# Four tiles' left-over rows of the experts' way down, taken together in 32-row products

## The chip, the cores and the metric

The kernel runs on one core of a Trainium2 chip. A core has a matrix engine (TensorE, PE in the profile; its weight loads are PEld), a vector engine (DVE), a scalar engine (ACT), a general engine (GpSimd, POOL) and a queue engine that issues DMAs (SyncE, SP). The engines run side by side, each in the order of its own instructions, and wait for one another with semaphores. Data lies in SBUF (128 partitions), and products go to PSUM, eight banks of 512 float32 values a partition. The metric is the device time of one execution, in microseconds (us).

## The reference

One decoder layer in float32 on 32 sequences of 128 tokens of width 512: self-attention with two softmaxes a head, cross-attention with rotary embeddings, and a mixture of experts with a shared expert. The change touches the experts alone:

```python
B, S, H = hidden_states.shape                     # 32, 128, 512
E, K = (NUM_EXPERTS, TOP_K)                       # 32 experts, 6 of them for each token
x = hidden_states.reshape(-1, H)                  # 4096 tokens
scores = jax.nn.sigmoid(x @ gate_w)
...                                               # the best 2 of 4 groups, then the best 6 experts
xs = x_exp[sort_idx]                              # 24576 rows, sorted by expert
g = jax.lax.ragged_dot(xs, w_gate, group_sizes)   # w_gate: 32 x 512 x 352
u = jax.lax.ragged_dot(xs, w_up, group_sizes)
d = jax.lax.ragged_dot(jax.nn.silu(g) * u, w_down, group_sizes)   # w_down: 32 x 352 x 512
expert_out = jnp.sum(out * weights[..., None], axis=1)
```

The inner width M is 352, which is two times 128 and 96.

## The kernel before

The stages follow one another: self-attention, cross-attention, routing, and then the experts, between groups of the shared expert. The routing sorts the rows into 192 tiles of 128 rows of one expert each (`usual`), and 8 shared tiles whose two halves of 64 rows belong to two experts (`mixed`). One shared tile stands after every 24 tiles, ahead of a tile whose number is a multiple of four.

An expert's weights lie in one of four sets of buffers (`SETS = 4`): tile i uses set i mod 4, and a load is skipped where the set holds the expert already (`cond=new`). `wg` and `wu` hold gate and up, `wd` holds the way down as three chunks of rows: 128, 128 and 96.

`Experts.run` writes the order of work out by hand, for PE, DVE, ACT and POOL, step by step. In step k of the loop:

- `gate_up(k)` (L1598): PE multiplies the tile's turned inputs `e_xT` by gate and up, four products of 128x352 each, into two PSUM banks; ACT takes silu of the first (L1602), DVE multiplies by the second into the one buffer `e_gu` (L1603).
- `turn_in_place(k)` (L1620): DVE turns two of the four 96-column parts of `e_gu` in 32x32 blocks, all 128 lanes at once, into `e_turned`.
- `turn_in(k + 2)` (L1584): DVE turns the fetched token rows `e_xr` of the tile two ahead into `e_xT`, four turns of 64x256. There are two buffers of `e_xT`.
- `turn_out(k)` (L1609): DVE turns the other two parts straight into their partitions of `e_guT`, eight turns of 32x96.
- `weights_in(k + 4)` (L1543): SP issues the loads of gate and up.
- `down(k - 2)` (L1637): PE multiplies `e_guT` by `wd`, three products of 512 columns, into one bank; ACT scales the result into `e_out` (L1641), and POOL issues the scatter that adds its rows to `sum_d` in HBM (L1644).
- `weights_out(k + 2)` (L1555, L1558): SP issues the two loads of `wd`.
- `move_out(k)` (L1627): ACT copies `e_turned` to its partitions of `e_guT`, eight copies.
- `tokens(k + 5)` (L1569): POOL issues two indirect fetches of token rows.

Every float32 product shows in the profile as two passes of PE, each with its own weight load. PSUM is handed out in pairs of banks, four pairs in turn (`Common.banks`). The shared tile's products use 64 columns of the array for each half. After the loop the engines pass a branch (L1831, further tiles if there are more than 192, which are none here), and the last groups of the shared expert follow (`Shared.group`, L1265 to L1304). These have 64 rows left over of 704 and take them for two blocks side by side (L1304). Cross attention has products of 32 rows and 512 columns, a head each, in different 32-row groups of the array (L690, L713).

Of the kernel before, what the change touches and what calls it, by code (L numbers as in the profile page):

```python
# [10 lines left out]
F32 = mybir.dt.float32  # L11
# [1303 lines left out]
class Experts:  # L1315
# [13 lines left out]
    RUN = 96  # L1329

    def __init__(
# [19 lines left out]
        self.wd = [cp.tile([P, len(M_CHUNKS), E], F32, name=f"wd{s}") for s in range(SETS)]  # L1351
# [92 lines left out]
    def fetch_halves(self):  # L1444
# [3 lines left out]
            self.p2.tile([P, len(M_CHUNKS), P], F32, name="e_guT", bufs=3)[0:32]  # L1448
# [98 lines left out]
    def weights_out(self, i):  # L1547

        if i not in self.expert:
            return  # L1550
        e, new = self.expert.pop(i)
        wd, src = self.wd[i % SETS], self.w_out[ds(e, 1)]
        top = (self.Q - 1) * 32
        m = (self.Q - 1) * self.RUN
        self.cm.nc.sync.dma_start(  # L1555
            out=wd[0:top], in_=src[:, 0:m, :].rearrange("o (p c) m -> p (o c) m", p=top), cond=new
        )
        self.last = self.cm.nc.sync.dma_start(  # L1558
            out=wd[top:P, 0:2, :], in_=src[:, m:M, :].rearrange("o (p c) m -> p (o c) m", c=2),
            cond=new,  # L1560
        )
# [43 lines left out]
    def turn_out(self, i):  # L1605
        t, half = self.guT[i], self.Q // 2
        for q in range(half):
            for s in range(self.Q):
                self.cm.nc.vector.transpose(t[ts(q, 32), :, ts(s, 32)], self.part(q, 3)[ts(s, 32)])  # L1609

    def part(self, q, n):
        return self.gu_s[:, ds(q * self.RUN, 32 * n)].rearrange("p (j c) -> p c j", c=n)

    def turn_in_place(self, i):
        half = self.Q // 2
        self.guT[i] = self.p2.tile([P, len(M_CHUNKS), P], F32, name="e_guT", bufs=3)
        z = self.turned[i] = self.p2.tile([P, half, len(M_CHUNKS), 32], F32, name="e_turned")
        for q in range(half, self.Q):
            n = min(self.RUN, M - q * self.RUN) // 32
            self.cm.nc.vector.transpose(z[:, q - half, 0:n], self.part(q, n))  # L1620

    def move_out(self, i):
        half, z, t = self.Q // 2, self.turned.pop(i), self.guT[i]
        for q in range(half, self.Q):
            n = min(self.RUN, M - q * self.RUN) // 32
            for s in range(self.Q):
                self.cm.nc.scalar.copy(t[ts(q, 32), 0:n, ts(s, 32)], z[ts(s, 32), q - half, 0:n])  # L1627

    def down(self, i):
        nc = self.cm.nc  # L1630
        py = self.cm.banks()[:, 0, :]
        t, last = self.guT.pop(i), len(M_CHUNKS) - 1
        both = [slice(0, P)] if i < self.n_tiles else [ts(h, P // 2) for h in range(2)]
        w = [self.wd[i % SETS]] if i < self.n_tiles else self.xd
        for c, (_, n) in enumerate(M_CHUNKS):
            for lanes, wd in zip(both, w):
                nc.tensor.matmul(  # L1637
                    py[lanes], t[:n, c, lanes], wd[:n, c, :], start=c == 0, stop=c == last
                )
        y = self.p3.tile([P, E], F32, name="e_out", bufs=4)  # L1640
        nc.scalar.mul(y, py, self.weight[:, i : i + 1])  # L1641
        m = i - self.n_tiles
        for into in [self.into[:, i : i + 1]] if m < 0 else [self.into_half[:, h, m : m + 1] for h in range(2)]:
            nc.gpsimd.indirect_dma_start(  # L1644
# [24 lines left out]
    def run(self):  # L1669
# [8 lines left out]
        with self.cm.tc.manual_schedule(engines={en.PE, en.DVE, en.Activation, en.Pool}):  # L1678
# [5 lines left out]
            for k in range(len(seq) + 2):  # L1684
# [5 lines left out]
                each(self.down, k - 2)  # L1690
                each(lambda i: self.weights_out(i + SETS), k - 2)
                each(self.move_out, k)
                if k < gap // 2 or k % 2:
                    next(loads, None)
                each(self.tokens, k + 5)
                m = seq[k - 2] - self.n_tiles + 1 if 2 <= k < len(seq) + 2 else 0
                if 0 < m < self.mixed:
                    loads = self.mixed_loads(m)
# [200 lines left out]
```

## Time and profile before

| | us |
|---|---|
| median of 3 runs | 3797.29 |
| lowest, highest | 3795.77, 3797.58 |
| the profiled execution, whole | 3800.08 |
| the profiled execution, span of instructions | 3798.3 |

The granted clock of PE was 0.992 of full speed over the span. The totals of the engines, and where the experts' tiles lie:

| stretch (us from the span's start) | PE busy | DVE busy | ACT busy | POOL busy |
|---|---|---|---|---|
| 2000 to 2100, the experts begin | 95.17 | 65.97 | 29.47 | 40.75 |
| 2100 to 2300 | 200.00 | 157.51 | 87.78 | 102.76 |
| 2900 to 3100 | 200.00 | 157.63 | 87.80 | 102.51 |
| 3300 to 3500, they end | 199.19 | 150.59 | 87.08 | 91.41 |
| 3500 to 3700, shared expert | 197.32 | 22.01 | 13.31 | 3.08 |

Busy time is the time in which an engine had at least one instruction in work. A row of the profile names the source line, the engine, the operation, the tiles (written <- read), the shape and the count; then come busy time and the mean length of one in ns, and the idle time before it with the engine that ended it. Matmuls overlap with their followers in the pipeline, so the step from one start to the next tells what a pass costs, and not its length. `32*128` ahead of a product's shape says how many rows and columns of the array it takes.

### The profile page before, as it was taken

The page shows a single profiled execution, that of the slowest core. Times are in us where ns is not written, and L with a number is a line of the kernel's source. Part 1 is how long each engine was busy: PE and PEld are TensorE (multiplying, and loading weights), DVE is VectorE, ACT ScalarE, POOL GpSimd, SP SyncE. Part 2 cuts the span into 40 slices and gives each one's busy share as a digit, 9 for nine tenths or more (in the row PEclk, how much of TensorE's full clock was granted, in tenths as well). Part 3 has the DMA queues.
Part 4 walks back from the last instruction along what each step waited for, and adds up shares of the span by engine and source line. Part 5 has one row for each costly group of instructions (what it writes and reads, how often), then busy time and mean ns, then how long its engine had stood idle before and what let it go on. Part 6 is the DMA issues. An engine that isn't in the chain of part 4 may idle for free. (4 is left out here: it accounts for less than half of the span.)

```text
span 3798.3 us, 59896 instructions
## 1 busy us (share of the span) xinstructions
PE 3717.0 (98%) x19060; PEld 1967.8 (52%) x19060; DVE 2677.8 (70%) x5402; ACT 2076.4 (55%) x5616; POOL 1917.2 (50%) x2154
## 2 busy tenths in 40 slices
PE   8999999899999999999999999999999999999999
PEld 5666666534444444444445555555555555555444
DVE  4888888877777778787326777777777777776111
ACT  6989998847677676776402444444444444443000
POOL 3555455545777777777424554555555555553000
PEclk9999999999999999999999999999999999999999
DMA  3111110121221111111135565656566665564210
GB/s 113 34 35 35 35 37 30 39 83 49 62 60 42 51 51 51 48 49 40 56 110 169 128 164 134 166 121 164 122 156 142 150 150 141 135 172 81 89 56 33
DMA packets 146548, 340.25 MB, mean 90 GB/s; under 512 B 28976, under 2 KB 33776, under 8 KB 146160
## 3 DMA queue, kind: packets, MB, share of 16 engines
q1 hardware_dynamic: 89408, 227.75, 18.8%
q0 software_dynamic: 55616, 107.79, 15.4%
q8 instruction: 154, 2.52, 0.3%
q14 instruction: 170, 1.39, 0.1%
q10 hardware_dynamic: 1200, 0.79, 0.1%
HBM read 574.59 MB, written 102.17 MB: 178 GB/s over the span
## 5 line engine op out<-in xcount | busy, mean ns | idle before, releaser
L694 DVE TENSOR_REDUCE nm<-ps 128x2 f32<-128x1024 f32 x512 | 610.6, 1214 | 113.2 <-PE ps L690 106.8
L717 ACT ACTIVATE xp<-ps 128x1024 f32<-128x1024 f32 x512 | 505.8, 1021 | 264.5 <-PE ps L690 202.7
L1644 POOL DMA_INDIRECT sum_d<-e_out,e_into x192 | 309.9, 1614 | 562.6 <-ACT e_out L1641 438.4
L713 PE MATMUL ps<-xqn,xk 32*128 32x512 f32 x2048 | 528.9, 621 | 20.7 <-ACT xp L717 19.1
L1637 PE MATMUL ps<-wd,e_guT 128*128 128x512 f32 (+1 forms) x1152 | 526.9, 593 | 0.3 <-ACT e_guT L1627 0.3
L690 PE MATMUL ps<-xk,xq 32*128 32x512 f32 x2048 | 526.9, 631 | 0.1
L1584 DVE STREAM_TRANSPOSE e_xT<-e_xr 64x256 f32<-64x256 f32 x800 | 499.5, 624 | 18.9 <-DMA e_xr<-h_d,e_run_of 10.7
L1609 DVE STREAM_TRANSPOSE e_guT<-e_gu 32x96 f32<-32x96 f32 x1600 | 477.7, 299 | 25.2
L1569 POOL DMA_INDIRECT e_xr<-h_d,e_run_of x400 | 413.8, 1035 | 159.7 <-issue 150.0
L1598 PE MATMUL ps<-wg,e_xT 128*128 128x352 f32 x1536 | 486.7, 459 | 0.0
L1598 PE MATMUL ps<-wu,e_xT 128*128 128x352 f32 x1536 | 485.7, 459 | 0.0
L1627 ACT COPY e_guT<-e_turned 32x96 f32<-32x96 f32 (+1 forms) x1600 | 407.1, 254 | 25.1 <-DVE e_turned L1620 3.9
L1598 PEld LDWEIGHTS ps<-wg,e_xT 128*128 128x128 f32 x1536 | 289.7, 189 | 217.8 <-issue 94.5
L278 ACT ACTIVATE s<-s,a_nm 128x128 f32<-128x128 f32 x1024 | 395.7, 396 | 5.2 <-DVE a_nm L264 5.2
L1598 PEld LDWEIGHTS ps<-wu,e_xT 128*128 128x128 f32 x1536 | 291.8, 190 | 162.6
L1641 ACT ACTIVATE e_out<-ps,e_weight 128x512 f32<-128x512 f32 x200 | 137.4, 687 | 411.8 <-PE ps L1637 409.5
L1637 PEld LDWEIGHTS ps<-wd,e_guT 128*128 128x128 f32 (+1 forms) x1152 | 218.5, 190 | 228.2 <-issue 188.5
L1602 ACT ACTIVATE e_act<-ps 128x352 f32<-128x352 f32 x200 | 92.6, 463 | 412.7 <-PE ps L1598 412.7
L713 PEld LDWEIGHTS ps<-xqn,xk 32*128 32x128 f32 x2048 | 169.0, 184 | 285.5 <-ACT xp L717 124.5
L1603 DVE TENSOR_TENSOR e_gu<-e_act,ps 128x352 f32<-128x352 f32 x200 | 104.1, 521 | 274.6 <-ACT e_act L1602 274.1
L728 PE MATMUL ps<-xp,v 128*32 128x512 f32 x2048 | 233.0, 595 | 7.9 <-ACT xp L717 7.9
L1031 POOL DMA_INDIRECT table_d<-entry,at x192 | 202.4, 1054 | 64.0 <-issue 52.9
(310 smaller groups left out, 5575.4 us busy)
## 6 DMA issues: line engine op xcount, KB each, us to landing
wg<-in_L_ffn_w_gate_dram SPq DMA_DIRECT2D x192, 704.0 KB
wu<-in_L_ffn_w_up_dram SPq DMA_DIRECT2D x192, 704.0 KB
wd<-in_L_ffn_w_down_dram SPq DMA_DIRECT2D x192, 576.0 KB
wd<-in_L_ffn_w_down_dram SPq DMA_DIRECT2D x192, 128.0 KB
xg<-in_L_ffn_w_gate_dram SPq DMA_DIRECT2D x16, 704.0 KB
xu<-in_L_ffn_w_up_dram SPq DMA_DIRECT2D x16, 704.0 KB
xd<-in_L_ffn_w_down_dram SPq DMA_DIRECT2D x16, 576.0 KB
xres<-in_x_dram SPq DMA_DIRECT2D x32, 256.0 KB
```

What stands on the lines that cost most here:

```text
L278: nc.scalar.activation(s[:, j, c, side, :], s[:, j, c, side, :], AF.Exp, bias=nm[n][:, side, at : at + 1], accum_out=sm[n][:, to : to + 1],)
L690: self.nc.tensor.matmul(sc[:, i, :], q[rows, ts(c, P)], k[rows, :], start=True, stop=True)
L694: self.nc.vector.tensor_reduce(at[:, self.ROW[side], 2 * pair : 2 * pair + 2], sc, AX.X, ALU.max, negate=True)
L713: self.nc.tensor.matmul(sc[:, i, :], k[rows, ts(c, P)], q[rows, :], start=True, stop=True)
L717: self.nc.scalar.activation(e, sc, AF.Exp)
L1569: self.cm.nc.gpsimd.indirect_dma_start(out=xr[:, t, :], out_offset=None, in_=self.h3_d.rearrange("t (h f) -> (t h) f", h=self.R), in_offse ...
L1584: self.cm.nc.vector.transpose(to[ts(w, half), :, v], xr[ts(v, half), w])
L1598: nc.tensor.matmul(pgu[lanes, half, 0:M], t[:, c, lanes], w[:, c, :], start=c == 0, stop=c == EC - 1,)
L1609: self.cm.nc.vector.transpose(t[ts(q, 32), :, ts(s, 32)], self.part(q, 3)[ts(s, 32)])
L1627: self.cm.nc.scalar.copy(t[ts(q, 32), 0:n, ts(s, 32)], z[ts(s, 32), q - half, 0:n])
L1637: nc.tensor.matmul(py[lanes], t[:n, c, lanes], wd[:n, c, :], start=c == 0, stop=c == last)
L1644: nc.gpsimd.indirect_dma_start(out=self.sum_d[:, :], out_offset=bass.IndirectOffsetOnAxis(ap=into, axis=0), in_=y[:, :], in_offset=None, b ...
```

## The change

The way down of a tile is split. Its first 256 rows are two full products, as before. Its last 96 rows are laid out over 32 partitions, three deep, in the 32-row group of the tile's set (its lane): partitions 32s to 32s + 31 for set s. The weights of these rows go to one buffer `wd_ends` for the four sets, and the turned activations of four tiles to one buffer `e_endT`. The way down is then done once for a group of four tiles: eight full products, and three rounds of four 32-row products, each in its own row group and into its tile's own PSUM bank, added to what the full products left there. It stands after the gate and up of the tile two behind the group's last one.

With it go these moves. The tile's columns are cut in four parts of 64 and one of 96. DVE turns parts 0 and 1 outward as 32x64 (eight turns), and three parts in place (two of 64 columns and the 96). ACT makes twelve copies for a tile instead of eight, the last four into the tile's lane of `e_endT`. `move_out` stands ahead of the way down in the step. The four results of a group leave together (`leave`), and the scatters are issued two a step from a list (`ready`). The loads of `wd` and `wd_ends` for the next four tiles are issued together after the group. The shared tiles keep their three products (`down_shared`).

```diff
@@ -1327,6 +1327,7 @@
     Q = 4
     R = 2
     RUN = 96
+    FULL, LEFT = 2, 3
 
     def __init__(
         self, cm, ctx, table_ds, h3_d, sum_d, w_gate, w_up, w_down, eid, fresh, rows, n_tiles,
@@ -1348,7 +1349,9 @@
         self.NT = rows.shape[1]
         self.wg = [cp.tile([P, EC, M], F32, name=f"wg{s}") for s in range(SETS)]
         self.wu = [cp.tile([P, EC, M], F32, name=f"wu{s}") for s in range(SETS)]
-        self.wd = [cp.tile([P, len(M_CHUNKS), E], F32, name=f"wd{s}") for s in range(SETS)]
+        self.wd = [cp.tile([P, self.FULL, E], F32, name=f"wd{s}") for s in range(SETS)]
+        self.ends = cp.tile([P, self.LEFT, E], F32, name="wd_ends")
+        self.py, self.endT = {}, {}
 
         self.gu_s = cp.tile([P, M], F32, name="e_gu")
 
...
@@ -1549,15 +1552,14 @@
         if i not in self.expert:
             return
         e, new = self.expert.pop(i)
-        wd, src = self.wd[i % SETS], self.w_out[ds(e, 1)]
-        top = (self.Q - 1) * 32
-        m = (self.Q - 1) * self.RUN
+        src, m = self.w_out[ds(e, 1)], self.FULL * P
         self.cm.nc.sync.dma_start(
-            out=wd[0:top], in_=src[:, 0:m, :].rearrange("o (p c) m -> p (o c) m", p=top), cond=new
+            out=self.wd[i % SETS],
+            in_=src[:, 0:m, :].rearrange("o (p c) m -> p (o c) m", p=P), cond=new,
         )
         self.last = self.cm.nc.sync.dma_start(
-            out=wd[top:P, 0:2, :], in_=src[:, m:M, :].rearrange("o (p c) m -> p (o c) m", c=2),
-            cond=new,
+            out=self.ends[ts(i % SETS, 32)],
+            in_=src[:, m:M, :].rearrange("o (p c) m -> p (o c) m", p=32), cond=new,
         )
 
     def tokens(self, i):
@@ -1602,46 +1604,86 @@
         nc.scalar.activation(act, pgu[:, 0, 0:M], AF.Silu)
         nc.vector.tensor_tensor(self.gu_s, act, pgu[:, 1, 0:M], ALU.mult)
 
+    def parts(self, i):
+
+        if i >= self.n_tiles:
+            t = self.guT[i]
+            return [(t, q, q * self.RUN, min(self.RUN, M - q * self.RUN) // 32) for q in range(self.Q)]
+        t, n = self.guT[i], self.FULL
+        return [(t, q, 32 * n * q, n) for q in range(self.Q)] + [
+            (self.endT[i // SETS], i % SETS, n * P, self.LEFT)
+        ]
+
+    def turn_in_place(self, i):
+
+        if i >= self.n_tiles:
+            self.guT[i] = self.p2.tile([P, len(M_CHUNKS), P], F32, name="e_guT", bufs=2)
+        else:
+            self.guT[i] = self.p3.tile([P, self.FULL, P], F32, name="e_mainT", bufs=7)
+            if i // SETS not in self.endT:
+                self.endT[i // SETS] = self.p3.tile([P, self.LEFT, P], F32, name="e_endT", bufs=2)
+        z = self.turned[i] = self.p2.tile([P, 3, len(M_CHUNKS), 32], F32, name="e_turned")
+        for k, (_, _, at, n) in enumerate(self.parts(i)[2:]):
+            self.cm.nc.vector.transpose(
+                z[:, k, 0:n], self.gu_s[:, ds(at, 32 * n)].rearrange("p (j c) -> p c j", c=n)
+            )
+
     def turn_out(self, i):
-        t, half = self.guT[i], self.Q // 2
-        for q in range(half):
+        for t, q, at, n in self.parts(i)[:2]:
+            cols = self.gu_s[:, ds(at, 32 * n)].rearrange("p (j c) -> p c j", c=n)
             for s in range(self.Q):
-                self.cm.nc.vector.transpose(t[ts(q, 32), :, ts(s, 32)], self.part(q, 3)[ts(s, 32)])
-
-    def part(self, q, n):
-        return self.gu_s[:, ds(q * self.RUN, 32 * n)].rearrange("p (j c) -> p c j", c=n)
-
-    def turn_in_place(self, i):
-        half = self.Q // 2
-        self.guT[i] = self.p2.tile([P, len(M_CHUNKS), P], F32, name="e_guT", bufs=3)
-        z = self.turned[i] = self.p2.tile([P, half, len(M_CHUNKS), 32], F32, name="e_turned")
-        for q in range(half, self.Q):
-            n = min(self.RUN, M - q * self.RUN) // 32
-            self.cm.nc.vector.transpose(z[:, q - half, 0:n], self.part(q, n))
+                self.cm.nc.vector.transpose(t[ts(q, 32), 0:n, ts(s, 32)], cols[ts(s, 32)])
 
     def move_out(self, i):
-        half, z, t = self.Q // 2, self.turned.pop(i), self.guT[i]
-        for q in range(half, self.Q):
-            n = min(self.RUN, M - q * self.RUN) // 32
+        z = self.turned.pop(i)
+        for k, (t, q, _, n) in enumerate(self.parts(i)[2:]):
             for s in range(self.Q):
-                self.cm.nc.scalar.copy(t[ts(q, 32), 0:n, ts(s, 32)], z[ts(s, 32), q - half, 0:n])
-
-    def down(self, i):
-        nc = self.cm.nc
+                self.cm.nc.scalar.copy(t[ts(q, 32), 0:n, ts(s, 32)], z[ts(s, 32), k, 0:n])
+
+    def down_shared(self, i):
+
         py = self.cm.banks()[:, 0, :]
         t, last = self.guT.pop(i), len(M_CHUNKS) - 1
-        both = [slice(0, P)] if i < self.n_tiles else [ts(h, P // 2) for h in range(2)]
-        w = [self.wd[i % SETS]] if i < self.n_tiles else self.xd
         for c, (_, n) in enumerate(M_CHUNKS):
-            for lanes, wd in zip(both, w):
-                nc.tensor.matmul(
+            for h, wd in enumerate(self.xd):
+                lanes = ts(h, P // 2)
+                self.cm.nc.tensor.matmul(
                     py[lanes], t[:n, c, lanes], wd[:n, c, :], start=c == 0, stop=c == last
                 )
+        return [(i, py)]
+
+    def down(self, tiles):
+
+        out = []
+        for i in tiles:
+            if i % 2 == 0:
+                pair = self.cm.banks()
+            t, py = self.guT.pop(i), pair[:, i % 2, :]
+            for c in range(self.FULL):
+                self.cm.nc.tensor.matmul(
+                    py, t[:, c, :], self.wd[i % SETS][:, c, :], start=c == 0, stop=False
+                )
+            out.append((i, py))
+        t = self.endT.pop(tiles[0] // SETS)
+        for c in range(self.LEFT):
+            for i, py in out:
+                rows = ts(i % SETS, 32)
+                self.cm.nc.tensor.matmul(
+                    py, t[rows, c, :], self.ends[rows, c, :], start=False, stop=c == self.LEFT - 1
+                )
+        return out
+
+    def leave(self, i, py):
+
         y = self.p3.tile([P, E], F32, name="e_out", bufs=4)
-        nc.scalar.mul(y, py, self.weight[:, i : i + 1])
+        self.cm.nc.scalar.mul(y, py, self.weight[:, i : i + 1])
+        return i, y
+
+    def scatter(self, i, y):
+
         m = i - self.n_tiles
         for into in [self.into[:, i : i + 1]] if m < 0 else [self.into_half[:, h, m : m + 1] for h in range(2)]:
-            nc.gpsimd.indirect_dma_start(
+            self.cm.nc.gpsimd.indirect_dma_start(
                 out=self.sum_d[:, :],
                 out_offset=bass.IndirectOffsetOnAxis(ap=into, axis=0),
                 in_=y[:, :],
@@ -1681,21 +1723,32 @@
             for k in range(2):
                 each(self.turn_in, k)
                 each(self.tokens, k + 3)
-            for k in range(len(seq) + 2):
+            ready, n = [], len(seq)
+            for k in range(n + 2):
                 each(self.gate_up, k)
                 each(self.turn_in_place, k)
                 each(self.turn_in, k + 2)
                 each(self.turn_out, k)
                 each(lambda i: self.weights_in(i + SETS), k)
-                each(self.down, k - 2)
-                each(lambda i: self.weights_out(i + SETS), k - 2)
                 each(self.move_out, k)
+                i = seq[k - 2] if k > 1 else 0
+                if i >= self.n_tiles:
+                    ready += [self.leave(*x) for x in self.down_shared(i)]
+                elif k > 1 and (i % SETS == SETS - 1 or i == self.end - 1):
+                    group = range(i // SETS * SETS, i + 1)
+                    ready += [self.leave(*x) for x in self.down(group)]
+                    for x in group:
+                        self.weights_out(x + SETS)
                 if k < gap // 2 or k % 2:
                     next(loads, None)
                 each(self.tokens, k + 5)
-                m = seq[k - 2] - self.n_tiles + 1 if 2 <= k < len(seq) + 2 else 0
-                if 0 < m < self.mixed:
-                    loads = self.mixed_loads(m)
+                for x in ready[:2]:
+                    self.scatter(*x)
+                del ready[:2]
+                if 0 <= i - self.n_tiles < self.mixed - 1:
+                    loads = self.mixed_loads(i - self.n_tiles + 1)
+            for x in ready:
+                self.scatter(*x)
 
 
 @with_exitstack
```

## The prediction

> **What bounds the kernel now.** I read the engine totals first, then the table of stretches over the expert stage, then the timeline of one tile there, then the rows of the two places that already run short products side by side.
>
> ```profile
> PE 3717.0 (98%) x19060; PEld 1967.8 (52%) x19060; DVE 2677.8 (70%) x5402; ACT 2076.4 (55%) x5616; POOL 1917.2 (50%) x2154
> 2100.00:3400.00 1300.00, 1300.00 (x4059) 729.57 (x4059) 1021.71 (x2658) 564.77 (x1775) 664.42 (x539) 1.00 0.61 146
> ```
>
> PE is busy for all 1300 us of this stretch at clock 1.00; DVE, the next, has 1021.71. So PE's own work sets the time here, and every hole in it would be seen. One tile, from the timeline (start, length, engine, line):
>
> ```profile
> 2701.16 2.53 PE L1598 MATMUL ps<-wg,e_xT 128*128 128x352 f32 x8
> 2703.53 2.53 PE L1598 MATMUL ps<-wu,e_xT 128*128 128x352 f32 x8
> 2705.89 2.74 PE L1637 MATMUL ps<-wd,e_guT 128*128 128x512 f32 x6
> 2706.65 0.52 DVE L1603 TENSOR_TENSOR e_gu<-e_act,ps 128x352 f32<-128x352 f32 x1 [1.34 <-ACT e_act L1602]
> 2707.20 0.44 DVE L1620 STREAM_TRANSPOSE e_turned<-e_gu 128x96 f32<-128x96 f32 x2
> 2707.57 2.54 DVE L1584 STREAM_TRANSPOSE e_xT<-e_xr 64x256 f32<-64x256 f32 x4
> 2708.47 2.53 PE L1598 MATMUL ps<-wg,e_xT 128*128 128x352 f32 x8
> 2710.13 2.48 DVE L1609 STREAM_TRANSPOSE e_guT<-e_gu 32x96 f32<-32x96 f32 x8
> 2713.21 2.74 PE L1637 MATMUL ps<-wd,e_guT 128*128 128x512 f32 x6
> ```
>
> From start to start: gate and up 2705.89-2701.16 = 4.73 us (16 passes, two to a product), the way down 2708.47-2705.89 = 2.58 (6 passes of 0.43), the tile 7.31. A pass over 96 rows takes the time of one over 128. DVE begins 0.76 after the last gate pass and is done at 2712.61; then it waits 1.34 for the next tile.
>
> ```profile
> 1203.70 0.70 PE L713 MATMUL ps<-xqn,xk 32*128 32x512 f32 x2
> 1203.71 0.70 PE L690 MATMUL ps<-xk,xq 32*128 32x512 f32 x2
> 1204.23 0.59 PE L713 MATMUL ps<-xqn,xk 32*128 32x512 f32 x2
> 1204.25 1.01 PE L690 MATMUL ps<-xk,xq 32*128 32x512 f32 x4
> 1204.68 0.59 PE L713 MATMUL ps<-xqn,xk 32*128 32x512 f32 x2
> 1205.09 0.59 PE L690 MATMUL ps<-xk,xq 32*128 32x512 f32 x2
> 1205.11 0.59 PE L713 MATMUL ps<-xqn,xk 32*128 32x512 f32 x2
> ...
> 3724.53 1.13 PE L1304 MATMUL ps<-sd,s_gu 64*128 64x512 f32 x4
> 3725.59 8.85 PE L1297 MATMUL ps<-sd,s_gu 128*128 128x512 f32 x20
> 3734.37 1.13 PE L1304 MATMUL ps<-sd,s_gu 64*128 64x512 f32 x4
> ```
>
> The first seven rows (cross attention) are 16 passes of 32 rows by 512 columns, four row groups at once: starts 0.53, then 0.43 and 0.43 apart. The last three are the shared experts' 64-row products. From 3724.53 to 3734.37 there are 9.84 us for 20 full passes and 4 half ones, two at a time: 22 x 0.429 = 9.44. So 0.40 us goes on changing the array's shape and back.
>
> **The change, part by part.** PE, the way down. Before, four tiles take 24 passes. After: 8 full products (16 passes) and 3 rounds of four 32-row products (6 pass times if four run abreast): 22 pass times, plus the change of shape 0.40 and some 0.02 of stagger between the four. Gain 2 x 0.429 - 0.42 = 0.44 us a group, 48 groups: **21.0 us**. Four abreast in four banks is shown above; adding into a bank is shown there only two abreast (L1304), hence the bounds: at the best no cost of shape, 41 us; at the worst two abreast, 6 more pass times a group, a loss of 2.1 us a group.
>
> The Trainium skill, page "TensorE: Matmul & The Clock Gate", in the table of its section on why this matters for kernels, speaks against the change: it gives 3.07x for four 32-row products of 512 columns. As an estimate by that page the 24 short passes would take 24/3.07 = 7.8 pass times where 8 are taken away, each group would lose 0.3 us with the change of shape, and the whole would end near 3832. The rows' steps of 0.43 for four decide here, since they are this chip's, with the same shape.
>
> DVE, what loses its cover. Before, each tile has 7.31 us between its gate passes and the next one's. After, PE runs four tiles' gates back to back (4.73 each) and then 9.84 of way down. In the built program the order on PE is gate 2, 3, 0, 1 of a group and then the way down of the four tiles that end two behind. DVE's order in a step stays: multiply (L1603), in-place turns (L1620), turn of the inputs two tiles ahead (L1584), outward turns (L1609). Call the four gates a, b, c, d: d needs the input turned in b's step. The step costs: multiply 0.55 (2706.65 to 2707.20); in-place turns 0.37 now for 96 and 64 columns, after for 64, 64 and 96, the second 64 at two fifths of it, 0.14: 0.51; inputs 2.56 (2707.57 to 2710.13), the last ready at 2.54; outward turns eight of 32x64 for eight of 32x96. These rows price them:
>
> ```profile
> L1609 DVE STREAM_TRANSPOSE e_guT<-e_gu 32x96 f32<-32x96 f32 x1418 | 423.5, 299 | 22.4
> L1620 DVE STREAM_TRANSPOSE e_turned<-e_gu 128x96 f32<-128x96 f32 x177 | 54.5, 308 | 6.1
> L1620 DVE STREAM_TRANSPOSE e_turned<-e_gu 128x64 f32<-128x64 f32 x177 | 35.6, 201 | 0.0
> L1627 ACT COPY e_guT<-e_turned 32x96 f32<-32x96 f32 x712 | 190.6, 268 | 10.7
> L1627 ACT COPY e_guT<-e_turned 32x64 f32<-32x64 f32 x709 | 171.0, 241 | 8.2
> ```
>
> The same operation falls from 308 to 201 ns with the columns; taken so, 2.48 becomes 1.65. A step is then 0.55 + 0.51 + 2.56 + 1.65 + 0.03 = 5.30, more than a gate's 4.73. Step a starts 4.73 + 0.76 = 5.49 after the group's start, step b at 10.79, its input is ready 0.55 + 0.51 + 2.54 = 3.60 later, at 14.39; d could start at 3 x 4.73 = 14.19. PE's load starts 0.05 after a DVE instruction that it waited for (L291, L308 and L713 in the trace), and that load is then bare (L713's first starts are 0.53 apart, not 0.43: 0.10), so the hole is 14.39 + 0.15 - 14.19 = **0.35 us**. After it the way down covers DVE again (step d ends near 26.6, the group near 29.1). 40 runs have it whole; in the eight with a shared tile among the four the gate of that tile is 0.15 longer (2.42 + 2.47 between its starts), so 0.20: 40 x 0.35 + 8 x 0.20 = **15.6 us**. Bounds: nothing (DVE early; PE cannot gain by that), and 1.06 a run, if the 32x64 turn falls only as ACT's copies do (268 to 241, so 0.27 each, 0.6 on the step) and the added in-place turn costs its full 0.20. I take 0.35, since the 128x64 row is the same operation on the same engine.
>
> Two ends. At the start six gates run back to back (no way down before the sixth): two further holes of 5.30 - 4.73, 1.1 us. At the end PE goes on only after ACT's branch, which comes after the last e_out: four of 0.69 at once instead of one, 2.1 later; a wait of 0.5 between the last two ways down goes: 1.6. Sum 2.7.
>
> ACT: 12 copies for 8, 8 x 0.25 + 4 x 0.28 = 3.1 us for 2.1, plus silu 0.46: 3.6 a step, under 4.73; step b's copies end near 14.8, c's silu is ready at 14.5 and its multiply at 16.1, so the 0.3 is hidden. The four e_out after the group (2.8) end before the next silu at 4.9. Without that cover the multiply slips with them.
>
> POOL: a scatter waits for the one before to land, 5.0 us from its issue, and now two stand in a row, twice a group; the token fetches behind them wait. From the way down's end: scatters at 1.3 and 6.4, tokens to 10.9, scatters at 11.4 and 16.5, tokens to 26.4, of 29. The first of these fetches lands (3.7) at 14.6 and is turned at 22.5. Hidden with 8 us to spare; with that gone, DVE's step would wait and PE with it.
>
> SP: the eight loads of w_down for four tiles are issued together after the way down instead of two a tile, ahead of the next gate loads; those are issued 24 us before use, as now. I cost them at nothing: in this stretch their queue moved 93.95 MB for 170 tiles of 2.1 MB, so most loads are skipped. Without that cover a late load would stop PE before a gate. PSUM: the two pairs are free again 3.1 us into the group, and asked for at 9.5.
>
> Sum: 21.0 - 15.6 - 2.7 = 2.7 us less than the profiled execution's 3800.08 (span 3798.3), which is 2.8 above the median of 3797.29: 3797.4 profiled, **3794.6** as a median.
>
> **Rivals.** (1) DVE keeps up: a hole under 0.25. For it: in-place turns of 128 lanes follow one another faster than their length (0.37 for 0.51). Against: the outward ones do not overlap (2.48 for 8 x 0.30). With no hole, 21.0 - 2.7: 3779. (2) The slower side: DVE's turns fall less than their columns, a hole of 1.06: 40 x 1.06 + 8 x 0.91 + 4 for the ends = 53.7 against 21.0: 3830. It decides from a hole of 0.56 on, which is a 32x64 turn of about 0.23. (3) The rounds run two abreast: 48 x 2.1 lost, and with the rest near 3916; against it, the 0.43 steps. (4) The scatter pairs starve the turns: each late fetch would show as a DVE wait of up to 3 us; with 48, some 3940; the 8 us to spare speak against it.
>
> **How the numbers follow.** 0.2% is 7.6 us, about what a measurement of this kernel can tell from no change. A hole of 0.25 to 0.56 keeps the time within it: 40 in 100, my forecast, with its own range 3790 to 3805. A smaller hole (1): 36. A larger one (2): 20. (3) 2 and (4) 2. The range leaves out the best ends, the upper part of (2), (3) and (4): 3778 to 3820.
>
> **What would show it.** The new products: sixteen full passes and then starts of four within 0.03 us, 0.43 apart, 0.10 bare at either end. The 32x64 turns near 201 ns. In every run of four gates one PE wait on DVE's e_xT of about 0.3 us before the fourth. No PE wait on ACT or DMA. I am wrong if that wait is absent, is over 0.6, stands before other gates too, or if the rounds' starts are 0.86 apart.

## The result, and the profile after

The changed kernel takes 3830.64 us (median of 6 runs, 3823.80 to 3835.11) against 3796.75 for the kernel before (6 runs, 3795.77 to 3797.58): a ratio of 1.0088, with a 95% interval of 1.0075 to 1.0101. It is slower by 33.9 us, where 2.7 us less were forecast, and it lies outside the range given (3778 to 3820).

The profiled execution took 3835.11 us and is the slowest of the six. Its totals, and the row of the table of stretches that answers to that of before (columns: sum of the stretch, then busy time and instructions of PE, PEld, DVE, ACT and POOL, then the granted clock, the DMA share and GB/s):

```profile
PE 3707.2 (97%) x19828; PEld 1944.6 (51%) x19828; DVE 2602.9 (68%) x5594; ACT 2243.5 (59%) x6384; POOL 1913.1 (50%) x2154
2100.00:3400.00 1300.00, 1265.39 (x4631) 695.23 (x4630) 935.88 (x2769) 697.92 (x2406) 646.73 (x527) 1.00 0.61 142
```

PE was busy for all of these 1300 us before and is now idle for 34.6 of them, at the same clock of 1.00. The expert stage, from the first gate pass to the first product of the shared expert after it (L1265), takes 1511.0 us where it took 1471.9, so 39.0 more; what lies ahead of it and behind it is the same within 3 us. The loss is all in this stage, and it shows as PE waiting.

A group of four tiles, from PE's timeline (start, length, engine, line; line numbers are the changed kernel's: L1600 is gate and up, L1663 the full products, L1671 the rounds):

```profile
2174.38 2.53 PE L1600 MATMUL ps<-wg,e_xT 128*128 128x352 f32 x8
2176.75 2.53 PE L1600 MATMUL ps<-wu,e_xT 128*128 128x352 f32 x8
2179.73 2.60 PE L1600 MATMUL ps<-wg,e_xT 128*128 128x352 f32 x8 [0.45 <-issue]
2182.17 2.53 PE L1600 MATMUL ps<-wu,e_xT 128*128 128x352 f32 x8
2184.53 7.03 PE L1663 MATMUL ps<-wd,e_mainT 128*128 128x512 f32 x16
2191.49 2.86 PE L1671 MATMUL ps<-wd_ends,e_endT 32*128 32x512 f32 x24
2194.28 2.63 PE L1600 MATMUL ps<-wg,e_xT 128*128 128x352 f32 x8
```

Two things are to be seen. First, the way down of four tiles takes 2194.28 - 2184.53 = 9.75 us, and 0.10 more because the pass after it starts on a bare load: 9.85 for 24 passes of 0.429, 10.30, of before. Second, the fourth gate starts 2.98 after the up before it and not 2.37: a hole of 0.61, and its own first weight load is bare as well, that is, not hidden behind a pass (2.44 to the next row for 2.37 elsewhere). DVE's timeline for the same steps says why:

```profile
2181.73 0.52 DVE L1605 TENSOR_TENSOR e_gu<-e_act,ps 128x352 f32<-128x352 f32 x1
2182.28 0.56 DVE L1627 STREAM_TRANSPOSE e_turned<-e_gu 128x64 f32<-128x64 f32 x3
2182.77 2.53 DVE L1586 STREAM_TRANSPOSE e_xT<-e_xr 64x256 f32<-64x256 f32 x4
2185.33 1.97 DVE L1635 STREAM_TRANSPOSE e_mainT<-e_gu 32x64 f32<-32x64 f32 x8
2187.40 0.52 DVE L1605 TENSOR_TENSOR e_gu<-e_act,ps 128x352 f32<-128x352 f32 x1
```

DVE does one step after another without a wait, 2187.40 - 2181.73 = 5.67 us for each, while a gate and up takes PE 4.73. (The input turns of the step before began at 2177.12 and took 2.51, so they ended at 2179.63, and the gate starts at 2179.73.) The groups of DVE's instructions price the turns (busy us, mean ns of one, idle ahead of them):

```profile
L1635 DVE STREAM_TRANSPOSE e_mainT<-e_gu 32x64 f32<-32x64 f32 x1328 | 310.9, 234 | 21.4
L1627 DVE STREAM_TRANSPOSE e_turned<-e_gu 128x64 f32<-128x64 f32 x341 | 63.4, 224 | 5.7
```

The 32x64 turn takes 234 ns where the 32x96 took 299: two thirds of the columns, 0.78 of the time.

The other holes are longer and not in every group. POOL's timeline (L1686 the scatters, L1571 the fetches of token rows), and three of the waits of the stretch from 2100 to 3400 (sum, count, longest):

```profile
2168.61 1.61 POOL L1686 DMA_INDIRECT sum_d<-e_out,e_into  x1 [0.30 <-issue]
2174.78 1.56 POOL L1686 DMA_INDIRECT sum_d<-e_out,e_into  x1 [4.56 <-ACT e_endT L1641]
2176.64 1.10 POOL L1571 DMA_INDIRECT e_xr<-h_d,e_run_of  x1 [0.30 <-DVE e_gu L1605]
2178.04 1.04 POOL L1571 DMA_INDIRECT e_xr<-h_d,e_run_of  x1 [0.31 <-issue]
2180.59 1.62 POOL L1686 DMA_INDIRECT sum_d<-e_out,e_into  x1 [1.51 <-ACT e_act L1604]
2189.73 1.57 POOL L1686 DMA_INDIRECT sum_d<-e_out,e_into  x1 [7.53 <-issue]
2191.61 1.09 POOL L1571 DMA_INDIRECT e_xr<-h_d,e_run_of  x1 [0.30 <-issue]
...
2199.61 1.61 POOL L1686 DMA_INDIRECT sum_d<-e_out,e_into  x1 [0.30 <-issue]
```

```profile
POOL sum_d L1686 <- DMA sum_d<-e_out,e_into: 179.6, 46, 8.0
ACT e_out L1679 <- DMA sum_d<-e_out,e_into: 33.9, 14, 5.4
DVE e_xT L1586 <- DMA e_xr<-h_d,e_run_of: 15.0, 9, 3.1
```

The second scatter of a pair stands on POOL until the first has landed, here 6.2 and 9.1 us after the first was issued, and six fetches in a row stand behind it. From the first scatter of this group to that of the next POOL needs 31.0 us, and a group of PE's is 29.5 long. Over the stage this distance lies between 26.5 and 35.6 us where no shared tile stands in between, and is over 29.5 in 17 of 37 cases. So POOL falls behind at times, and DVE waits for token rows and ACT for buffers of `e_out`. Where such a wait comes at the wrong step it reaches PE (DVE's row and PE's row of one such place):

```profile
2359.47 2.53 DVE L1586 STREAM_TRANSPOSE e_xT<-e_xr 64x256 f32<-64x256 f32 x4 [2.90 <-DMA e_xr<-h_d,e_run_of]
2362.10 2.61 PE L1600 MATMUL ps<-wg,e_xT 128*128 128x352 f32 x8 [2.51 <-issue]
```

The gate waits for the rows that DVE could turn only from 2359.47 on; PE stands 2.67 us. (The releaser "issue" is the profile's guess; the end of the turn 0.1 us before the gate is the evidence.) The stage has eight such long holes, six of them in this stretch, from 1.4 to 3.1 us. In six of the eight DVE waits for a fetch. The other two, before the gates at 2482.91 and 3459.89, come by another way: ACT stands 5.4 and 5.8 us for a buffer of `e_out`, so silu comes late, and with it DVE's multiply and the turn behind it. ACT's row and PE's row of the first:

```profile
2478.17 0.69 ACT L1679 ACTIVATE e_out<-ps,e_weight 128x512 f32<-128x512 f32 x1 [5.44 <-DMA sum_d<-e_out,e_into]
2482.91 2.59 PE L1600 MATMUL ps<-xg,e_xT 128*64 128x352 f32 x16 [2.42 <-DVE e_xT L1586]
```

### The profile page after: what moved, and what is told of

Its sections match the earlier page's. It is cut to its first block, busy times and chain, and to the rows that moved or that the text cites. A ratio compares the mean times of both kernels' runs of the same rounds, so it can differ in the third digit from the quotient of the medians.

```text
span 3833.4 us, 62104 instructions
## 1 busy us (share of the span) xinstructions
PE 3707.2 (97%) x19828; PEld 1944.6 (51%) x19828; DVE 2602.9 (68%) x5594; ACT 2243.5 (59%) x6384; POOL 1913.1 (50%) x2154
## 3 DMA queue, kind: packets, MB, share of 16 engines
q0 software_dynamic: 55616, 107.79, 15.6%
## 5 line engine op out<-in xcount | busy, mean ns | idle before, releaser
L1686 POOL DMA_INDIRECT sum_d<-e_out,e_into x192 | 304.6, 1587 | 623.5 <-issue 255.2
L1641 ACT COPY e_mainT<-e_turned 32x64 f32<-32x64 f32 x1536 | 370.6, 241 | 362.3 <-DVE e_turned L1627 346.8
L1600 PE MATMUL ps<-wg,e_xT 128*128 128x352 f32 x1536 | 499.2, 468 | 38.1 <-issue 35.0
L1571 POOL DMA_INDIRECT e_xr<-h_d,e_run_of x400 | 415.6, 1039 | 161.4 <-issue 120.6
L1600 PE MATMUL ps<-wu,e_xT 128*128 128x352 f32 x1536 | 485.7, 459 | 0.0
L1600 PEld LDWEIGHTS ps<-wg,e_xT 128*128 128x128 f32 x1536 | 284.1, 191 | 251.7 <-issue 62.7
L1635 DVE STREAM_TRANSPOSE e_mainT<-e_gu 32x64 f32<-32x64 f32 x1536 | 359.5, 234 | 24.7
L1600 PEld LDWEIGHTS ps<-wu,e_xT 128*128 128x128 f32 x1536 | 292.0, 190 | 162.8 <-issue 0.4
L1663 PE MATMUL ps<-wd,e_mainT 128*128 128x512 f32 x768 | 337.4, 592 | 0.0
L1679 ACT ACTIVATE e_out<-ps,e_weight 128x512 f32<-128x512 f32 x200 | 123.5, 687 | 193.2 <-PE ps L1671 140.4
L1663 PEld LDWEIGHTS ps<-wd,e_mainT 128*128 128x128 f32 x768 | 145.9, 190 | 170.9 <-issue 160.2
L227 POOL TENSOR_SCALAR k<-kz,a_keep,a_extra 128x256 f32<-128x256 f32 x128 | 82.2, 652 | 286.8 <-ACT kz L226 286.8
```

Of the source, the lines that this page charges most:

```text
L1571: self.cm.nc.gpsimd.indirect_dma_start(out=xr[:, t, :], out_offset=None, in_=self.h3_d.rearrange("t (h f) -> (t h) f", h=self.R), in_offse ...
L1600: nc.tensor.matmul(pgu[lanes, half, 0:M], t[:, c, lanes], w[:, c, :], start=c == 0, stop=c == EC - 1,)
L1635: self.cm.nc.vector.transpose(t[ts(q, 32), 0:n, ts(s, 32)], cols[ts(s, 32)])
L1663: self.cm.nc.tensor.matmul(py, t[:, c, :], self.wd[i % SETS][:, c, :], start=c == 0, stop=False)
L1686: self.cm.nc.gpsimd.indirect_dma_start(out=self.sum_d[:, :], out_offset=bass.IndirectOffsetOnAxis(ap=into, axis=0), in_=y[:, :], in_offset ...
```

## The experiments

Two theories for the loss. **Turns**: DVE's step is longer than a gate, so that the fourth gate of each run waits; this costs 0.69 us a group (0.62 of hole and 0.07 for the bare load), some 34 in all. **Scatters**: two in a row on POOL make the fetches and the buffers of `e_out` late; this costs some 20. Together they are 54 us; PE's own shorter way down gives some 20 of that back, and 34 are seen. The rival to the first is that the hole before the fourth gate is something else, a wait on ACT's copies or on the weights, as the releasers in the trace ("issue", ACT) would have it. The rival to the second is that the late fetches are only the turns' slack used up, so that they go when the turns are taken off the path.

### One scatter a step

```diff
-                for x in ready[:2]:
+                for x in ready[:1]:
                     self.scatter(*x)
-                del ready[:2]
+                del ready[:1]
```

> The changed kernel with one scatter a step from its list instead of two; all else as changed. Theory DVE (the fourth gate of a run waits 0.62 us for its turned input, and its first weight load is bare, 0.10: 47 x 0.72 = 34 us) expects these waits unchanged. Theory POOL (two scatters in a row, the second waiting some 5 us for the first to land, hold back the token fetches and the buffers of e_out; the nine waits of 1.4 to 3.1 us, the slow clock after them and 4 us at the end come from it) expects those to go: 20 to 28 us less, 3803 to 3811. If POOL is innocent: 3831.

Measured: 3810.94 us (3807.94 to 3813.69), ratio to before 1.0033 (1.0020 to 1.0046), so 19.7 less than the changed kernel. The waits, and the table row, of the same stretch:

```profile
POOL sum_d L1686 <- DMA sum_d<-e_out,e_into: 59.5, 33, 3.9
ACT e_out L1679 <- DMA sum_d<-e_out,e_into: 0.3, 1, 0.3
```

```profile
2100.00:3400.00 1300.00, 1281.33 (x4704) 704.89 (x4703) 944.48 (x2800) 707.07 (x2434) 660.79 (x537) 1.00 0.61 145
```

With two fetches between one scatter and the next, most of the time until a scatter has landed passes while POOL issues the fetches: POOL's waits that the profile puts down to a landing scatter fall from 179.6 to 59.5 us, the row of DVE's waits for fetches is gone, and the long holes of PE with it. What is left of PE's idle time, 18.7 us, is the regular hole before the fourth gate: 42 waits, each 0.6 from start to start and 0.45 as busy time counts it, since PE's busy time runs on a little past the last start. The whole stage has 49 of them; from start to start, with the bare loads behind them, they sum to 33.9 us. The scatters' share of the loss is 20 us.

### Turns of the inputs three tiles ahead

A third buffer of `e_xT`, and the turns of the inputs (and the fetches) one step earlier. Then the fourth gate needs what DVE turned in the first step and not in the second.

```diff
...
-        xT = self.xT[i] = self.p2.tile([P, EC, P], F32, name="e_xT")
+        pool = self.p3 if self.turned_in % 3 == 2 else self.p2
+        self.turned_in += 1
+        xT = self.xT[i] = pool.tile([P, EC, P], F32, name="e_xT")
...
-            for k in range(2):
+            for k in range(3):
...
-                each(self.turn_in, k + 2)
+                each(self.turn_in, k + 3)
...
-                each(self.tokens, k + 5)
+                each(self.tokens, k + 6)
```

> The changed kernel with a third buffer of e_xT: inputs are fetched and turned one tile earlier, so that the fourth gate's input is turned in the first gate's step; DVE's work and the scatters are as changed. Theory DVE expects the waits of 0.62 us to vanish, some 30 us less: 3797 to 3803, with waits for late fetches left. If the holes came from PE itself or from POOL alone: within 5 us of 3831.

Measured: 3787.30 us (3783.88 to 3790.84), 0.9972 (0.9961 to 0.9983): 43.3 less than the changed kernel, more than the turns alone should give. The regular hole is gone, and of the late fetches most are too, though the scatters still stand in pairs: DVE's waits for fetches sum to 31.4 us in the stretch, twice those of the changed kernel, and PE is busy for 1298.32 of 1300. A turn that is a step earlier than its gate can be late without PE seeing it. At the end of the stage the pairs still cost: PE waits 11.4 us there for ACT's branch, and 6.6 with one scatter a step.

Both edits together:

> Both edits, the third buffer and one scatter a step. If the two theories together explain the loss, what is left is the change of PE alone: two passes less a group (41 us), shape changes 0.40 a group (19 us more), some 3 us more at the end: 3776 to 3782. If a third cause is at work: 3790 or more.

Measured: 3777.11 us (3774.77 to 3779.19), 0.9944 (0.9928 to 0.9961). The gates of a run of four, and the table row:

```profile
2199.28 2.53 PE L1602 MATMUL ps<-wg,e_xT 128*128 128x352 f32 x8
2201.65 2.53 PE L1602 MATMUL ps<-wu,e_xT 128*128 128x352 f32 x8
2204.02 2.53 PE L1602 MATMUL ps<-wg,e_xT 128*128 128x352 f32 x8
2206.38 2.53 PE L1602 MATMUL ps<-wu,e_xT 128*128 128x352 f32 x8
2100.00:3400.00 1300.00, 1300.00 (x4820) 720.10 (x4819) 968.88 (x2870) 722.89 (x2488) 672.46 (x546) 1.00 0.62 149
```

All starts are 2.37 apart, PE is busy for the whole stretch, and the stage takes 1452.4 us, 19.5 less than before the change. The same two edits compared step by step: turns ahead alone take 43.3, and one scatter then 10.2 more (by the two profiled executions some 5 of it at that last wait); one scatter alone takes 19.7, and turns ahead then 33.8 more. The causes overlap by 9.5 us. Since one_scatter leaves no late fetches in PE's way, its 33.8 are the price of the turns by themselves.

The same edit of the turns on the kernel before, to see whether it is worth anything without the change:

> The kernel before, with the third buffer of e_xT and inputs fetched and turned one tile earlier, as a control. Theory DVE (the buffer pays only where gates stand back to back) expects no difference, since every tile there has 1.34 us of idle DVE and a way down between its gates: within 3 us of the kernel before. If the buffer is worth something by itself: 10 us less or more.

Measured: 3797.67 us (3795.35 to 3800.97), 1.0001 (0.9992 to 1.0011). Nothing, so the 33.8 us are a cost that the change brought, and ahead_one's gain over before is the change's own.

### Half of the way down between the gates

The other way to give DVE its cover: the full products of the group's first two tiles after the second gate, the rest after the fourth, so that only two gates ever follow one another. `down` is cut in two (`down_full`, `down_ends`); one scatter a step as above.

```diff
                 elif k > 1 and (i % SETS == SETS - 1 or i == self.end - 1):
                     group = range(i // SETS * SETS, i + 1)
-                    ready += [self.leave(*x) for x in self.down(group)]
+                    out = half + self.down_full(group[2:])
+                    ready += [self.leave(*x) for x in self.down_ends(out)]
+                    self.cm.banks()
                     for x in group:
                         self.weights_out(x + SETS)
+                elif k > 1 and i % SETS == 1:
+                    half = self.down_full(range(i - 1, i + 1))
```

> The changed kernel with its eight full products in two halves, the first two tiles' four products two steps before the rest, so that never more than two gates stand back to back (but at the start); one bank pair is passed over in each group so that no gate waits for e_out; one scatter a step; only two buffers of e_xT, DVE's work as changed. Theory DVE expects no waits on turned inputs: 3774 to 3782, faster than before. If only a third buffer could help (a matter of buffers, not of cover): 3805 or more.

Measured: 3777.99 us (3775.82 to 3781.10), 0.9949 (0.9933 to 0.9966), the same as ahead_one within the runs' spread, by another edit that leaves the turns and their buffers alone. PE's timeline:

```profile
2182.45 3.60 PE L1663 MATMUL ps<-wd,e_mainT 128*128 128x512 f32 x8
2185.98 2.86 PE L1675 MATMUL ps<-wd_ends,e_endT 32*128 32x512 f32 x24
2188.77 2.63 PE L1600 MATMUL ps<-wg,e_xT 128*128 128x352 f32 x8
...
2198.34 3.60 PE L1663 MATMUL ps<-wd,e_mainT 128*128 128x512 f32 x8
2201.77 2.53 PE L1600 MATMUL ps<-wg,e_xT 128*128 128x352 f32 x8
```

Two gates are 9.57 us, and 3.43 of products follow: 13.0 for two steps of DVE's 5.67. Two independent ways of giving DVE time remove the same 33 us.

### The outward turns longer by half

The four turns of the first outward part are done twice, which changes no value, once on one_scatter and once on ahead_one.

```diff
-        for t, q, at, n in self.parts(i)[:2]:
+        for t, q, at, n in self.parts(i)[:1] + self.parts(i)[:2]:
```

> The kernel with one scatter a step, and four of each tile's eight outward turns done twice with the same result (4 x 0.247 = 0.99 us more on DVE a tile, 192 tiles, 190 us of work in all). Theory DVE: the wait before the fourth gate grows by the 0.99 us of one step, from 0.62 to 1.61 us; 47 x 0.99 = 46 us more than one_scatter, some 3857. If DVE's length did not set the wait: 3811.

Measured: 3861.65 us (3860.76 to 3863.40), 1.0168 (1.0151 to 1.0185): 50.7 more than one_scatter, where 46 were expected. The wait before the fourth gate:

```profile
2186.92 2.53 PE L1600 MATMUL ps<-wu,e_xT 128*128 128x352 f32 x8
2190.95 2.60 PE L1600 MATMUL ps<-wg,e_xT 128*128 128x352 f32 x8 [1.50 <-ACT e_mainT L1641]
```

4.03 from start to start, so the hole is 1.67 where it was 0.62. From multiply to multiply DVE's step is 6.70 us here (2187.31 to 2194.01) for 5.67: its extra 1.03 us goes into the hole one for one, and 49 such waits make 50.5 us. The releaser named here is ACT, but ACT had nothing more to do in this kernel; the hole follows DVE.

> The same additional turns in the kernel with the third buffer and one scatter a step. A DVE step is then 6.5 us, four are 26 of the group's 28.8, and the input that a gate needs is turned a step earlier. Theory DVE: the added 190 us of work cost nothing, within 5 us of 3777. If DVE is the bound there already: 3820.

Measured: 3778.75 us (3775.72 to 3779.82), 0.9949 (0.9932 to 0.9965), 1.6 more than ahead_one, within the spread of either. DVE carries 170 us more in the stretch, and PE doesn't see it:

```profile
2100.00:3400.00 1300.00, 1300.00 (x4819) 720.14 (x4818) 1139.50 (x3593) 724.15 (x2493) 674.59 (x547) 1.00 0.61 149
```

So the same turns cost 50.7 us or nothing, depending on when their neighbour, the turn of the inputs, is due.

### What the rounds cost

On ahead_one, the rounds are left out: the last 96 rows of the way down are not computed.

```diff
-                    py, t[:, c, :], self.wd[i % SETS][:, c, :], start=c == 0, stop=False
+                    py, t[:, c, :], self.wd[i % SETS][:, c, :], start=c == 0, stop=c == self.FULL - 1
...
-        for c in range(self.LEFT):
+        for c in range(0):
```

> The kernel with the third buffer and one scatter a step, without the three rounds of 32-row products (the last 96 rows of the way down are left out; all else stays, the turns, copies and loads of them too). It measures the rounds by what goes: six pass times of 0.429 and the change of shape 0.37 to 0.40, 2.95 us a group, 48 groups, 142 us less: 3635. Two abreast would have cost 5.5 us a group: 3512.

Measured, in one run: 3644.22 us, 132.9 less than ahead_one. In the trace the stage is 134.2 shorter, although PE's wait at its end is 6.8 longer (13.4) and two waits of 1.8 in all are new; without these three 142.8, or 142.8 / 48 = 2.97 us a group. Six pass times of 0.429 are 2.57; the other 0.40 is the change of shape, as read from the shared expert's rows. And the group's way down without rounds, 6.86 us for 16 passes:

```profile
2194.60 7.03 PE L1665 MATMUL ps<-wd,e_mainT 128*128 128x512 f32 x16
2201.46 2.53 PE L1602 MATMUL ps<-wg,e_xT 128*128 128x352 f32 x8
```

### The end of the stage

In split_one PE waits 6.8 us at the stage's end for ACT's branch, where the kernel before waited 3.2:

```profile
PE ps L1265 <- ACTq L1831: 3.2, 1, 3.2
```

The last `e_out` waits for a buffer, which comes free only when a scatter of the group before has landed; ACT stands 1.74 us for it in split_one. On split_one, `e_out` gets a fifth buffer, and `e_mainT`, which needs fewer with the way down split, gives up two.

```diff
-            self.guT[i] = self.p3.tile([P, self.FULL, P], F32, name="e_mainT", bufs=7)
+            self.guT[i] = self.p3.tile([P, self.FULL, P], F32, name="e_mainT", bufs=5)
...
-        y = self.p3.tile([P, E], F32, name="e_out", bufs=4)
+        y = self.p3.tile([P, E], F32, name="e_out", bufs=5)
```

> The kernel with the way down in two parts and one scatter a step, with five buffers of e_out instead of four (and five of e_mainT instead of seven, which is what the split needs). At the end of the experts' stage the last e_out waits for the scatter of the group before to land, and PE stands 6.7 to 6.9 us there, against 3.2 in the kernel before. With a fifth buffer that wait should go: 1 to 2 us less than split_one, 3776 to 3777. If the four e_out in a row are what keeps PE: no difference, 3778.

Measured: 3776.93 us (3774.29 to 3777.93), 0.9942 (0.9929 to 0.9956). The wait at the end of split_one, and then of this kernel:

```profile
PE ps L1265 <- ACTq L1892: 6.8, 1, 6.8
```

```profile
PE ps L1265 <- ACTq L1892: 4.8, 1, 4.8
```

The wait is 2.0 us shorter, as it should be. The time is 1.1 less than split_one's, and the runs of the two overlap, so the gain is seen in the trace and not settled in the time. This kernel and ahead_one are faster by some 20 us than the kernel before, and by more than 50 than the change as it was made.

## Why the prediction was wrong

The terms of the prediction's sum, beside what the runs gave:

| step of the prediction | forecast, us | measured, us | from |
|---|---|---|---|
| PE, the way down | -21.0 | -21.6 | 48 x (10.30 - 9.85) |
| DVE, what loses its cover, with the start | +15.6 + 1.1 | +33.8 | one_scatter against ahead_one |
| the end | +1.6 | +2.9 | PE's last wait in one_scatter, 6.6 for 3.2, less the 0.5 that goes |
| POOL | 0 | +19.7 | the changed kernel against one_scatter |
| sum | -2.7 | +34.8 | 33.9 as a whole |

**PE, the way down: right.** The rounds run as forecast: the six fours (three rounds of two passes) start 0.43 apart but for the first step of 0.53, the four of each lie within 0.02 us, and the gate after them has a bare load of 0.10 again. The two bounds, no cost of shape and two abreast, are both excluded. The stage of ahead_one is 19.5 shorter than before, with 3.4 more of wait at its end; of these 22.9 the 0.5 between the last two ways down is a wait that goes, so 22.4 are PE's own work. The page of the Trainium skill that was weighed against the rows ("TensorE: Matmul & The Clock Gate", in its section on why this matters for kernels) has four 32-row products at 3.07 times the rate; as an estimate by it the 24 short passes would take 3.35 us a group, and with the shape change 3.75. no_rounds shows 2.97 with the shape change in it: 10.30 / 2.97 = 3.5 times with it, and 4.0 without. The measurement decides, and the row taken was the better guide. That the estimate of the whole by that page, near 3832, lies at the measured time is chance: the rounds cost what the rows said, and the loss came from elsewhere.

**DVE, what loses its cover: the mechanism right, its size half of what came.** The place, the waiting gate, the engine and the arithmetic hold; the failing term is the one price "taken so, 2.48 becomes 1.65". It carried the ratio of the 128-lane in-place turns (308 to 201 ns) over to the 32-lane turns. Those take 1.97 for eight, and DVE's gap after them is 0.10 and not 0.03, so the step is 5.67 and not 5.30. Nearly all of this 0.37 falls into the hole: 0.69 with the bare load where 0.35 was forecast, which more_turns_one confirms from the other side (1.03 us of DVE's step, 1.05 of hole). The row of ACT's copies, which gave the upper end (0.27 a turn), erred the other way, with 1.06 of hole (by its own terms, 0.58 for the eight turns and 0.06 for the one in place, it would have been 0.99). By the prediction's own sum a hole of 0.69 gives 40 x 0.69 + 8 x 0.54 + 2.7 - 21.0 = 13.6 more than before, 3811; one_scatter, which has this loss alone, measured 3810.94. The deciding point that rival 2 named, 0.56 of hole or a turn of 0.23, was passed.

**POOL: the step that failed as a mechanism.** "Hidden with 8 us to spare" was worked out with pairs 5.1 us apart and one group by itself. In the trace the second scatter of a pair starts 6.5 us after the first on average (median 5.75, up to 10.4). The scatters land no later than before; the last number of these rows, before and after, is the median from issue to landing:

```profile
sum_d<-e_out,e_into POOLq DMA_INDIRECT x171, 5.0
sum_d<-e_out,e_into POOLq DMA_INDIRECT x167, 4.9
```

The forecast took this median for every scatter. It left out the 0.8 us from a landing to the start of the second scatter (0.77 to 0.80 wherever the trace tells the landing), and the scatters that land late: in the kernel before, where each has two fetches behind it, the mean is 5.5 and the longest 9.9. That a late one holds up POOL is thus the pair's doing.

From the first scatter to the end of the last fetch the group shown takes 30.7 us, where the forecast had 25.1 (1.3 to 26.4), and a shared tile adds a pair of its own. Where a group takes longer than PE's 29.5, nothing is to spare, and its delay is passed on to the next. Rival 4 had the right mechanism and 2 in 100; it priced it at 3 us in every group, and it came in eight places of the stage, two of them by ACT's buffers and not by the fetches, 20 us in all. That the measured time agrees with rival 2's 3830 is chance: the hole was 0.69 and not its 1.06, and the rest is the scatters.

**The ends: too small.** At the start three waits of 0.57, 0.86 and 0.88 came for the two of 0.57. At the end PE's wait grew from 3.2 to 7.4, and in one_scatter to 6.6:

```profile
PE ps L1265 <- ACTq L1884: 7.4, 1, 7.4
```

The forecast counted ACT's four results but not the buffers that they go to: four buffers, and the fourth of them free only after a scatter of the group before. ACT's row of the fourth in the changed kernel:

```profile
3535.45 0.69 ACT L1679 ACTIVATE e_out<-ps,e_weight 128x512 f32<-128x512 f32 x1 [2.03 <-DMA sum_d<-e_out,e_into]
```

**SP and PSUM: nothing, as forecast; ACT: its own work nothing, its buffers not.** No wait of PE that a load of weights or a bank ends shows in the stretch. ACT's waits for `e_out`, 33.9 us in the stretch, which the forecast did not have, made two of the stage's long holes; they went with the scatter pairs (0.3 us in one_scatter). The signs named in advance serve: the regular hole stood before the fourth gate alone, as said, but at 0.6 it was at the mark given for being wrong, the 32x64 turn was 234 ns and not near 201, and DVE and ACT waited on DMA, and PE on them.

What stays open: why some scatters need 7 to 10 us to land, before the change as after it. Fetches, weight loads and scatters are under way at the same time, and no run here separates them.

## What to carry to other kernels

When work that stood between the steps of a bottleneck engine is gathered into one block, the engines beside it lose their cover in the stretch without it: compare the period of each of them there, not over the stage, with the bottleneck's, and give the input that is due first one more buffer and one more step of lead before anything else (33.8 us here for one buffer). A small instruction's price is to be taken from the same partition count, since a ratio from another shape was off by a fifth, and that doubled the hole. An engine that issues transfers which wait for one another is a queue: two such in a row stopped all that stood behind them (19.7 us here), and with two fetches between them PE's long holes were gone.

## What the runs showed of the hardware that was not expected

- DVE's 32x32-block turns cost about as much on 32 partitions as on 128: 32x64 takes 234 ns (0.247 us from start to start), 128x64 takes 224, 32x96 takes 297 to 299, 128x96 268 to 308. Per value the wide turn is some four times cheaper.
- After two long waits PE's next passes were slow. The row below and another at 3459.89 follow waits of 3.06 and 2.78 us: five passes of 352 columns 0.587 us apart and not 0.296, so 4.13 to the next row for 2.44 elsewhere. After the wait of 2.67 at 2362.10 (shown above) the gate took its usual 2.44. The granted clock is 0.50 for 3.41 us from 3388.87 on and for 3.41 us from 3460.55 on, and 1.00 from 2362 to 2366. The slow passes cost 1.7 us each time on top of the wait.

```profile
3388.79 4.30 PE L1600 MATMUL ps<-wg,e_xT 128*128 128x352 f32 x8 [2.89 <-issue]
3392.92 2.53 PE L1600 MATMUL ps<-wu,e_xT 128*128 128x352 f32 x8
```

- The Trainium skill, page "TensorE: Matmul & The Clock Gate", in Part 1, has a cold clock of half speed after an idle window of about 3.4 us, on a free-running window. The halved steps and the granted clock of 0.50 agree; here they already follow an idle time of 2.78 us. The two slow stretches are each 3.41 us long and begin 71.68 us apart, 21 times that. By steps of 3.41 us back from them, the wait of 2.67 lies across a boundary (2361.5), and the two others nearly whole within one step; whether the length of a wait or its place decides, no run here separates.
- The changed kernel's runs spread over 11 us, where 13 runs of the kernel before beside each other spread over 5, and with one scatter a step it is 6. That the waits for transfers make the difference is likely and not shown.
